# Attention rows with the second bias inside the exponential, key halves added before the sums, and a new order within a row

## The chip, the core and the metric

The kernel runs on one core of one Trainium2 chip. The metric is the device time of one execution in microseconds (us): the median of three runs before the change is 3339.98 us (3334.67 to 3347.28).

A core has five engines with queues of their own: TensorE (PE in the profile; its weight loads are PEld), VectorE (DVE), ScalarE (ACT), GpSimd (POOL) and SyncE (SP), which here issues most of the transfers. Each engine works through its instructions in order; semaphores make one wait for another. PE writes to PSUM; DVE and ACT read PSUM and SBUF, POOL works on SBUF tiles here.

## The reference

The model has two layers. The change concerns layer 0 alone, which is attention along rows with a gate. `x` and `kv_x` are 256 x 256 x 128 (rows s, positions, channels), with 4 heads of 32 channels:

```python
q = split_heads(einsum('...qi,oi->...qo', q_x, wq)) / sqrt(32)   # q_x is the group-normalised x
k = split_heads(einsum('...ki,oi->...ko', kv_x, wk))
v = split_heads(einsum('...ki,oi->...ko', kv_x, wv))
a = einsum('bshqd,bshkd->bshqk', q, k)
a = a + bias1 + bias2           # bias1: (1, 1, 4, 256, 256); bias2: (1, 256, 1, 1, 256)
a = softmax(a, axis=-1)
o = einsum('bshqk,bshkd->bshqd', a, v)
g = sigmoid(einsum('...qi,oi->...qo', q_x, wg) + bg)
x = x + einsum('...qi,oi->...qo', o * g, wo) + bo
```

`bias1` depends on head, query and key and is the same for all rows; `bias2` depends on row and key. The group normalisation needs statistics over all of `x` before the first row. Layer 1 then works on the result with Fourier transforms, a second attention and several normalisations.

## The kernel before

**Stages.** `layer0` first loads `x` in 32 blocks of 1 MB, transposes them on PE and takes statistics on DVE (L113, L114), sums them up (L116 to L119), and then calls `layer0_rows`. That one first prepares the biases: it loads `bias1` and `bias2` (L170, L172), takes their largest and smallest values for a later test (L174, L175), transposes them (L180, L191), and leaves `b1T` (keys on the partitions; heads 0 and 1 as they are, heads 2 and 3 already through the exponential) and `eb2`, the exponential of `bias2` times a constant. The test at the end (L124 to L146) sends the whole layer through a slow general branch when a bias is out of its limits or the result isn't finite.

**A row.** The row loop goes over 256 rows. Row `i` passes through steps that are spread over several iterations, so that iteration `i` issues `scores(i)`, `turn(i+2)`, `project(i+1)`, `attend(i-1)`, `out(i-2)` and `spectrum(i-3)`:

- `load`: two rows of `x` and `kv` at a time, on SP's queue (tiles `xt`, `kt`), four rows or more ahead.
- `turn`: PE transposes both (tile `tr`); ACT writes `xnT` (L219, normalised) and `kvT` (L221).
- `project`: PE makes queries and keys (tile `qk`) and gate and values (tile `gv`); ACT copies `qkT` (L230), DVE writes `v`, the values times `eb2` (L240), ACT the gate by a tanh (L244).
- `scores`: 8 small matmuls with 32 rows each, one for each head and key half (tiles `sc`, two PSUM tiles with one buffer each). Heads 2 and 3 go through ACT's exponential (L261) and are then multiplied by the exponential of `bias1` on POOL (L263); heads 0 and 1 get `bias1` added by DVE (L262, reading PSUM) and then ACT's exponential (L264). Each of these works on 1024 elements per partition.
- `attend`: 8 matmuls with the values, and 8 with `eb2` in the place of the values, which give the softmax's sums (tile `av`, L275). A matmul of this type stands in the profile as two records. DVE multiplies by the gate (L281) and takes the reciprocal of the sums (L282); POOL multiplies the two (`og`, L284) and adds the output bias to `x` (`xb`, L287).
- `out`: PE projects (tile `wo`), DVE adds `xb` (L297), SP stores the row (L300).
- `spectrum`: PE transposes the row and multiplies it by a Fourier matrix (tile `u`); DVE takes statistics (L311), ACT copies the spectrum to `U` (L312).

**What sets the order.** The program writes the order out by hand; a scheduler places the instructions in each engine's queue by their dependencies, and inserts the semaphores. PSUM tiles `tr`, `qk`, `gv`, `av`, `wo` and `u` share a pool of four buffers that go round in the order in which they are asked for: a tile can be written when the tile four before it has been read out. SP's queue holds loads of later rows and stores of earlier ones in one order.

Of the kernel before, what the change touches and what calls it, by code (L numbers as in the profile page):

```python
# [63 lines left out]
DEN_SCALE = 2.0 ** -69  # L64
BIAS_MAX, BIAS_MIN = 12.0, -40.0


def layer0(tc, I, C, ident, x1d, U, stats2):

# [8 lines left out]
    with ExitStack() as ctx:  # L78
        const = ctx.enter_context(tc.tile_pool(name="l0c", bufs=1))
        wT = {}  # L80
# [3 lines left out]
        nc.sync.dma_start(bg, I["L0_conv_bg"].unsqueeze(1))  # L84
        bad = const.tile([P, 4], FP, name="bad")
        adft = const.tile([P, 2, 129], FP, name="adft")
        nc.sync.dma_start(adft, C["adft"].rearrange("(p j) f -> p j f", j=2))

        with tc.tile_pool(name="l0p", bufs=2) as pp, tc.tile_pool(
            name="l0pp", bufs=4, space=PSUM  # L90
        ) as ps_p:
            gavg = pp.tile([P, P], FP, name="gavg", bufs=1)
            nc.sync.dma_start(gavg, C["gavg"])
            for n in ("wq", "wk", "wv", "wg", "wo"):
                w = pp.tile([P, P], FP, tag="w", name="w_" + n)
                nc.sync.dma_start(w, I["L0_conv_" + n])
                ps = ps_p.tile([P, 512], FP, tag="a", name="wps_" + n)
                nc.tensor.transpose(ps[:, 0:P], w, ident)
                wT[n] = const.tile([P, P], FP, name="wT_" + n)
                if n == "wq":  # L100
                    nc.scalar.mul(wT[n], ps[:, 0:P], 1.0 / math.sqrt(32.0))
                else:
                    nc.scalar.copy(wT[n], ps[:, 0:P])

            stats = pp.tile([P, NS // 2, 6], FP, name="stats1", bufs=1)
            xr = x.rearrange("s q c -> (s q) c").rearrange("(b p n) c -> b p n c", p=P, n=16)
            for b in range(xr.shape[0]):
                xb = pp.tile([P, 16, P], FP, tag="xb", name=f"xb_{b}", bufs=4)
                nc.sync.dma_start(xb, xr[b])
                for t in range(4):  # L110
                    ps = ps_p.tile([P, 512], FP, tag="a", name=f"xps_{b}_{t}")
                    for k in range(4):
                        nc.tensor.transpose(ps[:, k * P : (k + 1) * P], xb[:, 4 * t + k, :], ident)  # L113
                    nc.vector.bn_stats(stats[:, b * 4 + t, :], ps)  # L114
            mv = pp.tile([P, 2], FP, name="mv1", bufs=1)
# [5 lines left out]
        layer0_rows(tc, I, ident, x1d, U, stats2, wT, mr, nmr, bg, adft, bad)  # L121

        with tc.tile_pool(name="l0f", bufs=1) as fp, tc.tile_pool(
# [7 lines left out]
            nc.vector.tensor_reduce(f[:, 1:2], bad[:, 0:2], AX.X, ALU.max)  # L131
            nc.vector.tensor_scalar(f[:, 1:2], f[:, 1:2], BIAS_MAX, None, ALU.is_le)
            nc.vector.tensor_reduce(f[:, 2:3], bad[:, 2:4], AX.X, ALU.min)
            nc.vector.tensor_scalar(f[:, 2:3], f[:, 2:3], BIAS_MIN, None, ALU.is_ge)
            nc.vector.tensor_mul(f[:, 0:1], f[:, 0:1], f[:, 1:2])
            nc.vector.tensor_mul(f[:, 0:1], f[:, 0:1], f[:, 2:3])
# [12 lines left out]
def layer0_rows(tc, I, ident, x1d, U, stats2, wT, mr, nmr, bg, adft, bad):  # L149
# [3 lines left out]
    nc = tc.nc  # L153
    x, kv = I["x"][0], I["L0_conv_kv_x"][0]
    NS = x.shape[0]
    SG = 2
    with ExitStack() as ctx:
        const = ctx.enter_context(tc.tile_pool(name="l0r", bufs=1))
        wo = const.tile([P, P], FP, name="wo_half")
        nc.vector.tensor_scalar(wo, wT["wo"], 0.5, None, ALU.mult)  # L160
        hbg = const.tile([P, 1], FP, name="hbg")
        nc.vector.tensor_scalar(hbg, bg, 0.5, None, ALU.mult)
        bo = const.tile([P, P], FP, name="bo")
        nc.sync.dma_start(bo, I["L0_conv_bo"].partition_broadcast(P))

        b1T = const.tile([P, 4, 2, 256], FP, name="b1T")
        eb2 = const.tile([P, 2, NS], FP, name="eb2")
        with tc.tile_pool(name="l0b", bufs=2) as bp, tc.tile_pool(name="l0bp", bufs=4, space=PSUM) as ps_b:
            b1n = bp.tile([P, 4, 2, 256], FP, name="b1n", bufs=1)
            nc.sync.dma_start(b1n, I["L0_conv_bias1"][0, 0].rearrange("h (p j) k -> p h j k", j=2))  # L170
            b2n = bp.tile([P, 2, 256], FP, name="b2n", bufs=1)
            nc.sync.dma_start(b2n, I["L0_conv_bias2"][0, :, 0, 0, :].rearrange("(j p) k -> p j k", p=P))  # L172
            for k, (op, at) in enumerate(((ALU.max, 0), (ALU.min, 2))):
                nc.vector.tensor_reduce(bad[:, at : at + 1], b1n.rearrange("p h j k -> p (h j k)"), AX.X, op)  # L174
                nc.vector.tensor_reduce(bad[:, at + 1 : at + 2], b2n.rearrange("p j k -> p (j k)"), AX.X, op)  # L175
            for h in range(4):
                ps = ps_b.tile([P, 512], FP, tag="a", name=f"b1ps_{h}")
                for c in range(2):
                    for j in range(2):
                        nc.tensor.transpose(  # L180
                            ps[:, (2 * c + j) * P : (2 * c + j + 1) * P], b1n[:, h, j, c::2], ident
                        )
                dst = b1T[:, h].rearrange("p c q -> p (c q)")
                if h < 2:
                    nc.vector.tensor_copy(dst, ps)
                else:
                    nc.scalar.activation(dst, ps, AF.Exp)
            ps = ps_b.tile([P, 512], FP, tag="a", name="b2ps")
            for c in range(2):
                for j in range(2):  # L190
                    nc.tensor.transpose(  # L191
                        ps[:, (2 * c + j) * P : (2 * c + j + 1) * P], b2n[:, j, c::2], ident
                    )
            nc.scalar.activation(eb2.rearrange("p c s -> p (c s)"), ps, AF.Exp)
            nc.vector.tensor_scalar(eb2, eb2, DEN_SCALE, None, ALU.mult)

        ld = ctx.enter_context(tc.tile_pool(name="l0ld", bufs=2))
# [3 lines left out]
        rows = {}  # L201

        def load(g):
            s0 = g * SG
            xt = ld.tile([P, SG, 2, P], FP, tag="xt", name=f"xt_{g}", bufs=4)
            nc.sync.dma_start(xt, x[s0 : s0 + SG].rearrange("s (p j) c -> p s j c", j=2))
            kt = ld.tile([P, SG, 2, P], FP, tag="kt", name=f"kt_{g}")
            nc.sync.dma_start(kt, kv[s0 : s0 + SG].rearrange("s (p j) c -> p s j c", j=2))
            for i in range(SG):
                rows[s0 + i] = {"x": xt[:, i], "kv": kt[:, i]}  # L210

        def turn(s):
# [6 lines left out]
            nc.scalar.activation(r["xnT"], ps[:, 0:256], AF.Identity, bias=nmr, scale=mr[:, 1:2])  # L219
# [3 lines left out]
        def project(s):  # L223
# [8 lines left out]
            for c in range(2):  # L232
# [5 lines left out]

            r["v"] = wk.tile([P, 2, P], FP, tag="v", name=f"v_{s}", bufs=3)
            nc.vector.tensor_tensor(  # L240
                r["v"], ps[:, 256:512].rearrange("p (c d) -> p c d", c=2), bc(eb2[:, :, s], 2, P), ALU.mult
            )
            r["gate"] = wk.tile([P, 256], FP, tag="gate", name=f"gate_{s}", bufs=3)
            nc.scalar.activation(r["gate"], ps[:, 0:256], AF.Tanh, bias=hbg, scale=0.5)  # L244
# [74 lines left out]
        for i in range(NS + 3):  # L319
# [6 lines left out]
            if i + 1 < NS:  # L326
                project(i + 1)
# [1190 lines left out]
```

## Time and profile before

| what | us |
|---|---|
| median of three runs | 3339.98 |
| the profiled execution, its own time | 3339.29 |
| its span in the profile | 3337.5 |
| statistics of `x`: last DVE statistic ends | 95.02 |
| first transpose of a row starts | 119.84 |
| last `U` copy of a row ends | 1812.83 |
| layer 1, the rest of the span | 1524.7 |

Busy time over the span, from the first part of the page: PE 2903.5 (87%), DVE 1874.7 (56%), ACT 1258.2 (38%), POOL 1107.9 (33%). These shares are means over stages. In the second part, the span is cut into 40 slices of 83 us, one digit each for tenths of busy time:

```
PE   7799999999999999999997795879976595688666
DVE  8566666666666666666666215736563253355344
ACT  0355555555555555555553101010001431244022
POOL 0255555555555555555553002000000700000001
PEclk9899999999999999999998975889987797799766
```

The rows are slices 2 to 22. There PE is busy all the time (9 means 90% or more), the others about half. Idle time of an engine that isn't the bottleneck costs nothing; so what counts in the rows is what PE does and what makes it wait.

Costliest groups of the row loop (256 of each per execution, except where noted; mean of one in ns): the reciprocal L282 on DVE, 1750; the multiply L263 on POOL, 2382; the bias add L262 on DVE, 1206; the exponentials L261 and L264 on ACT, 1060 and 1078; the gate multiplies L281 on DVE, 421, and L284 on POOL, 728.

### The profile page before, as it was taken

How to read it: one execution, taken by the hardware profiler on the slowest of the kernel's cores; microseconds unless marked ns; L12 is line 12 of the kernel's file. 1: busy time of each engine (PE TensorE's matmuls, PEld its weight loads, DVE VectorE, ACT ScalarE, POOL GpSimd, SP SyncE). 2: the span in 40 equal slices, each digit the busy share in tenths (PEclk: the TensorE clock that was granted, in tenths of full speed). 3: DMA queues.
4: the chain of work that ended last, by engine and by line, in shares of the span. 5: the costliest groups of instructions: out<-in, count | busy, mean ns of one | idle time of the engine just before them, and what ended most of it. 6: DMA issues, size and time to landing. Idle time of an engine off the chain costs nothing. (4 is left out here: it accounts for less than half of the span.)

```text
span 3337.5 us, 71936 instructions
## 1 busy us (share of the span) xinstructions
PE 2903.5 (87%) x30049; PEld 1942.7 (58%) x30049; DVE 1874.7 (56%) x2852; ACT 1258.2 (38%) x2293; POOL 1107.9 (33%) x919
## 2 busy tenths in 40 slices
PE   7799999999999999999997795879976595688666
PEld 6577777777777777777775474744433244333443
DVE  8566666666666666666666215736563253355344
ACT  0355555555555555555553101010001431244022
POOL 0255555555555555555553002000000700000001
PEclk9899999999999999999998975889987797799766
DMA  9221221222221221222120000077633924887398
GB/s 378 96 63 59 63 63 60 61 63 60 61 63 60 62 63 60 61 63 61 60 63 27 1 8 13 0 277 251 226 129 125 312 74 113 269 308 275 86 358 319
DMA packets 237710, 401.71 MB, mean 120 GB/s; under 512 B 25125, under 2 KB 184312, under 8 KB 223304
## 3 DMA queue, kind: packets, MB, share of 16 engines
q1 hardware_dynamic: 221832, 329.97, 30.7%
q0 software_dynamic: 12672, 46.14, 3.5%
q10 hardware_dynamic: 2880, 20.97, 1.5%
q8 instruction: 238, 3.90, 0.5%
q14 instruction: 88, 0.72, 0.1%
HBM read 261.20 MB, written 135.79 MB: 119 GB/s over the span
## 5 line engine op out<-in xcount | busy, mean ns | idle before, releaser
L263 POOL TENSOR_TENSOR e<-e,b1T 128x1024 f32<-128x1024 f32 x256 | 609.8, 2382 | 103.7 <-ACT e L261 103.5
L282 DVE RECIPROCAL rd<-av 128x256 f32<-128x256 f32 x256 | 448.1, 1750 | 0.0
L284 POOL TENSOR_TENSOR og<-t,rd 128x256 f32<-128x256 f32 x256 | 186.4, 728 | 611.7 <-PE sc L253 593.5
L312 ACT COPY U<-u 128x129 f32<-128x129 f32 x256 | 99.3, 388 | 719.3 <-DVE stats L311 719.3
L281 DVE SCALAR_TENSOR_TENSOR t<-gate,av 128x256 f32<-128x256 f32 x256 | 107.7, 421 | 401.0 <-ACT gate L244 383.4
L262 DVE TENSOR_TENSOR e<-sc,b1T 128x1024 f32<-128x1024 f32 x256 | 308.8, 1206 | 2.7 <-PE sc L253 2.6
L253 PE MATMUL sc<-qkT 32*128 32x256 f32 x4096 | 293.4, 400 | 0.1
L264 ACT ACTIVATE e<-e 128x1024 f32<-128x1024 f32 x256 | 276.0, 1078 | 0.5 <-DVE e L262 0.4
L275 PE MATMUL av<-e,v 128*32 128x256 f32 x4096 | 274.7, 385 | 0.5 <-POOL e L263 0.5
L261 ACT ACTIVATE e<-sc 128x1024 f32<-128x1024 f32 x256 | 271.4, 1060 | 4.0 <-PE sc L253 3.8
L275 PE MATMUL av<-e,eb 128*32 128x256 f32 x4096 | 268.2, 379 | 0.0
L1025 PE MATMUL yps<-xt,mpT 128*128 128x512 f32 x512 | 230.3, 603 | 13.3 <-DMA xt<-x1d 13.3
L1351 POOL DMA_DIRECT2D out_dram<-x x64 | 34.1, 533 | 621.1 <-DVE x L1350 314.6
L287 POOL TENSOR_TENSOR xb<-xt,bo 128x256 f32<-128x256 f32 x256 | 187.5, 733 | 118.9 <-DMA kt<-in_L_conv_kv_x_dram 118.9
L240 DVE TENSOR_TENSOR v<-gv,eb 128x256 f32<-128x256 f32 x256 | 108.9, 425 | 198.3 <-PE gv L237 198.2
L1187 POOL TENSOR_TENSOR ww<-ww,xw 128x1024 f32<-128x1024 f32 x24 | 56.4, 2351 | 493.1 <-DMA xw<-x1d 482.3
L253 PEld LDWEIGHTS sc<-qkT 32*128 32x128 f32 x4096 | 185.0, 184 | 37.9 <-issue 0.7
L293 PEld LDWEIGHTS wo<-wo_half,og 128*128 128x128 f32 x1024 | 133.5, 190 | 107.0 <-issue 104.2
L275 PEld LDWEIGHTS av<-e,eb 128*32 128x32 f32 x4096 | 133.0, 110 | 88.2
L293 PE MATMUL wo<-wo_half,og 128*128 128x128 f32 x1024 | 182.4, 301 | 1.9 <-POOL og L284 1.9
L275 PEld LDWEIGHTS av<-e,v 128*32 128x32 f32 x4096 | 106.8, 109 | 129.7 <-ACT xnT L219 80.5
L1025 PEld LDWEIGHTS yps<-xt,mpT 128*128 128x128 f32 x512 | 95.4, 191 | 125.6 <-issue 113.6
(599 smaller groups left out, 5479.5 us busy)
## 6 DMA issues: line engine op xcount, KB each, us to landing
xb<-in_x_dram SPq DMA_DIRECT2D x32, 1024.0 KB
xt<-in_x_dram SPq DMA_DIRECT2D x128, 256.0 KB
kt<-in_L_conv_kv_x_dram SPq DMA_DIRECT2D x128, 256.0 KB
x1d<-x SPq DMA_DIRECT2D x256, 128.0 KB
xt<-x1d SPq DMA_DIRECT2D x32, 1024.0 KB
out_dram<-x POOLq DMA_DIRECT2D x64, 512.0 KB, 7.6
yd<-yt ACTq DMA_DIRECT2D x20, 1024.0 KB
x<-x1d SPq DMA_DIRECT2D x40, 512.0 KB
```

The lines of the kernel that those rows point to most:

```text
L240: nc.vector.tensor_tensor(r["v"], ps[:, 256:512].rearrange("p (c d) -> p c d", c=2), bc(eb2[:, :, s], 2, P), ALU.mult)
L253: nc.tensor.matmul(sc[h // 2][:, h % 2, c * 256 : (c + 1) * 256], qkT[p, 256 + c * P : 256 + (c + 1) * P], qkT[p, 0:256], start=True, stop ...
L261: nc.scalar.activation(e[1], s1[1], AF.Exp)
L262: nc.vector.tensor_tensor(e[0], s1[0], b1[0], ALU.add)
L263: nc.gpsimd.tensor_tensor(e[1], e[1], b1[1], ALU.mult)
L264: nc.scalar.activation(e[0], e[0], AF.Exp)
L275: nc.tensor.matmul(ps[hd, den * 256 : (den + 1) * 256], w, r["e"][h // 2][:, h % 2, c, :], start=(c == 0), stop=(c == 1),)
L282: nc.vector.reciprocal(rd, ps[:, 256:512])
L284: nc.gpsimd.tensor_tensor(r["og"], t, rd, ALU.mult)
L287: nc.gpsimd.tensor_tensor(r["xb"], r["x"], bc(bo, 1, 2), ALU.add)
L293: nc.tensor.matmul(ps[:, j * P : (j + 1) * P], r["og"][:, j * P : (j + 1) * P], wo, start=True, stop=True)
L1025: nc.tensor.matmul(ps[j].rearrange("p (n w) -> p n w", w=W), mpT[:, sc, tt], by_turn(xt[:, sc])[:, j], start=(sc == 0), stop=False,)
```

## The change

The bias handling is turned round. All four heads are treated alike: ACT's exponential takes `bias2` as its bias, a value for each partition (key), so that each 1024-wide exponential becomes two 512-wide ones, one for each key half, and `b1T` holds the exponential of `bias1` (times a constant) for all heads. A new step, `weigh`, multiplies the exponentials by it, heads 2 and 3 on POOL, heads 0 and 1 on DVE, and then adds the two key halves (`es`). The sums in `attend` are then 4 matmuls with a tile of ones instead of 8 with `eb2`. The values are only copied (L256 of the new kernel). The last gate multiply goes from POOL to DVE (L309), in place into `og`, and the addition of the output bias writes `x1` directly (L312). Constants keep the numbers in range: 2^-46 in `b1T`, 2^34 in the gate multiply, the rest in `wo`.

In an iteration the order is now `scores(i)`, `turn(i+2)`, `project(i+1)`, `weigh(i)`, `out(i-3)`, `spectrum(i-4)`, `attend(i-1)`, and the loop has one more turn. The PSUM pool still has four buffers. The biases' limits are taken from `b1T` in rows 8 to 15 (8 reduces on DVE), and `bias2` has no limits any more. The preparation (transposes, exponentials, copies) and the loads of the weights are moved into the loop over the 32 blocks of `x`, and the first four rows' loads stand behind it. The class `Rows` holds what were local variables. The diff, cut to its core:

```diff
-DEN_SCALE = 2.0 ** -69
-BIAS_MAX, BIAS_MIN = 12.0, -40.0
+E_SCALE, SUM_SCALE = 2.0 ** -46, 2.0 ** 34
+WO_SCALE = 0.5 / SUM_SCALE
+BIAS_MAX, BIAS_MIN = 24.0, -40.0
...
+                if b == 2:
+                    nc.sync.dma_start(gavg, C["gavg"])
...
+                    for n in ("wq", "wk", "wv", "wg", "wo"):
+                        w = pp.tile([P, P], FP, tag="w", name="w_" + n)
+                        nc.sync.dma_start(w, I["L0_conv_" + n])
...
+                if b == 8:
+                    rows.prepare(pp, ps_p)
+            rows.load(0)
+            rows.load(1)
...
+    def prepare(self, bp, ps_b):
+        nc, I, ident = self.tc.nc, self.I, self.ident
+        nc.gpsimd.memset(self.ones, 1.0)
...
+            dst = self.b1T[:, h].rearrange("p c q -> p (c q)")
+            nc.scalar.activation(dst, ps, AF.Exp)
+            nc.gpsimd.tensor_scalar(dst, dst, E_SCALE, None, ALU.mult)
...
+        nc.scalar.copy(self.b2T.rearrange("p c s -> p (c s)"), ps)
...
-            nc.vector.tensor_tensor(
-                r["v"], ps[:, 256:512].rearrange("p (c d) -> p c d", c=2), bc(eb2[:, :, s], 2, P), ALU.mult
-            )
+            nc.vector.tensor_copy(r["v"].rearrange("p c d -> p (c d)"), ps[:, 256:512])
...
-            nc.scalar.activation(e[1], s1[1], AF.Exp)
-            nc.vector.tensor_tensor(e[0], s1[0], b1[0], ALU.add)
-            nc.gpsimd.tensor_tensor(e[1], e[1], b1[1], ALU.mult)
-            nc.scalar.activation(e[0], e[0], AF.Exp)
+            for hp in (1, 0):
+                for c in range(2):
+                    nc.scalar.activation(
+                        r["e"][hp][:, :, c, :], sc[hp][:, :, c * 256 : (c + 1) * 256],
+                        AF.Exp, bias=b2T[:, c, s : s + 1],
+                    )
+
+        def weigh(s):
...
+            for hp, eng in ((1, nc.gpsimd), (0, nc.vector)):
+                e = r["e"][hp]
+                e1 = e.rearrange("p h c q -> p (h c q)")
+                eng.tensor_tensor(e1, e1, b1T[:, 2 * hp : 2 * hp + 2].rearrange("p h c q -> p (h c q)"), ALU.mult)
+                eng.tensor_tensor(r["es"][hp], e[:, :, 0, :], e[:, :, 1, :], ALU.add)
...
+            for h in range(4):
+                nc.tensor.matmul(
+                    ps[32 * h : 32 * h + 32, 256:512], self.ones, r["es"][h // 2][:, h % 2, :],
+                    start=True, stop=True,
+                )
...
             nc.vector.reciprocal(rd, ps[:, 256:512])
-            r["og"] = wk.tile([P, 256], FP, tag="og", name=f"og_{s}")
-            nc.gpsimd.tensor_tensor(r["og"], t, rd, ALU.mult)
+            nc.vector.scalar_tensor_tensor(t, rd, SUM_SCALE, t, ALU.mult, ALU.mult)
...
-        for i in range(NS + 3):
+        for i in range(NS + 4):
...
+            if i < NS:
+                weigh(i)
+            if 8 <= i < 16:
+                k, h = divmod(i - 8, 4)
+                nc.vector.tensor_reduce(
...
+            if 0 <= i - 3 < NS:
+                out(i - 3)
+            if 0 <= i - 4 < NS:
+                spectrum(i - 4)
+                del rows[i - 4]
             if 0 <= i - 1 < NS:
                 attend(i - 1)
-            if 0 <= i - 2 < NS:
-                out(i - 2)
-            if 0 <= i - 3 < NS:
-                spectrum(i - 3)
-                del rows[i - 3]
```

The line numbers of the new kernel's steps that the prediction names: L236 `xnT`, L238 `kvT`, L247 `qkT`, L258 gate, L275 the exponentials, L287 the multiplies by `b1T`, L288 the added halves, L307 to L309 gate and reciprocal, L322 `x1`, L336 statistics, L337 `U`.

## The prediction

> **What bounds the kernel now.** I read four views, in this order: the busy times by stretch (which stage, which engine), the timeline of one row (what waits for what), the groups (durations), and the timelines of a later stage where GpSimd and VectorE work side by side. In the first view the columns after the length are PE, PEld, DVE, ACT and POOL busy, then granted clock, DMA share and GB/s.
>
> ```profile
> 400.00:800.00 400.00, 400.00 (x4387) 288.00 (x4386) 258.14 (x366) 228.50 (x426) 230.68 (x182) 1.00 0.20 61
> ```
>
> TensorE has no idle time in the row loop, at full clock; DVE works 65%, ACT 57%, POOL 58%. One row, from the timeline (start, duration, engine, line):
>
> ```profile
> 1002.37 1.15 PE L253 MATMUL sc<-qkT 32*128 32x256 f32 x16
> 1003.45 0.33 PE L216 MATMUL tr<-ident,xt 128*128 128x128 f32 x1
> 1004.22 1.06 ACT L261 ACTIVATE e<-sc 128x1024 f32<-128x1024 f32 x1
> 1005.17 0.56 ACT L219 ACTIVATE xnT<-tr,nmr,mr 128x256 f32<-128x256 f32 x1
> 1005.61 0.37 ACT L221 COPY kvT<-tr 128x256 f32<-128x256 f32 x1
> 1005.78 1.07 PE L275 MATMUL av<-e,v 128*32 128x256 f32 x16
> 1006.67 1.05 PE L275 MATMUL av<-e,eb 128*32 128x256 f32 x16
> 1006.82 0.59 ACT L230 COPY qkT<-qk 128x512 f32<-128x512 f32 x1
> 1007.29 0.51 ACT L244 ACTIVATE gate<-gv,hbg 128x256 f32<-128x256 f32 x1
> 1007.64 0.71 PE L293 MATMUL wo<-wo_half,og 128*128 128x128 f32 x4
> 1008.19 0.38 PE L306 MATMUL u<-ident,x 128*128 128x128 f32 x2
> 1008.95 1.15 PE L253 MATMUL sc<-qkT 32*128 32x256 f32 x16
> ```
>
> A row is 1008.95 - 1002.37 = 6.58 us. From start to start PE spends 1.08 on the scores, 0.49 on transposes, 1.84 on projections (1003.94 to 1005.78), 0.89 on values, 0.97 on sums, 0.55 on `wo` and 0.76 on `u`. Note kvT: it ends at 1005.98, and the matmul that takes over its PSUM buffer, `wo`, starts 1.66 later. Durations for the new work:
>
> ```profile
> L263 POOL TENSOR_TENSOR e<-e,b1T 128x1024 f32<-128x1024 f32 x256 | 609.8, 2382 | 103.7 <-ACT e L261 103.5
> L287 POOL TENSOR_TENSOR xb<-xt,bo 128x256 f32<-128x256 f32 x256 | 187.5, 733 | 118.9 <-DMA kt<-in_L_conv_kv_x_dram 118.9
> L1064 DVE TENSOR_TENSOR xm_11r<-F,mixwr 128x1024 f32<-128x1024 f32 x1 | 1.2, 1226 | 0.5 <-PE xacc L1067 0.5
> L1064 DVE TENSOR_TENSOR z0m_10r<-F,mixwr 128x512 f32<-128x512 f32 x1 | 0.7, 693 | 0.2 <-PE z0acc L1067 0.2
> ```
>
> And two engines beside each other, in layer 1:
>
> ```profile
> 2041.54 0.40 DVE L820 TENSOR_SCALAR qt<-Xlo,kwi,hs 128x256 f32<-128x256 f32 x1
> 2043.59 0.46 DVE L823 SCALAR_TENSOR_TENSOR qf<-Xlo,kwr,qt 128x256 f32<-128x256 f32 x1
> 2043.97 1.13 DVE L820 TENSOR_SCALAR qt<-Xlo,kwi,hs 128x256 f32<-128x256 f32 x1
> 2043.76 1.20 POOL L851 TENSOR_TENSOR pr<-pr,st 128x512 f32<-128x512 f32 x1 [0.70 <-DVE st L850]
> L826 POOL TENSOR_SCALAR qt<-Xlo,kwr x16: 914/954/1405, 2027.7 to 2070.5; 128x256 f32<-128x256 f32 x16
> ```
>
> The same DVE operation takes 0.40 alone and 1.13 when a two-input POOL operation runs: it ends 0.14 after POOL. POOL's L851 takes 1.04 alone and 1.20 when it starts under a two-input DVE operation (L823); POOL's L826 grows from 0.91 to 1.41. Against a full block: most two-input DVE operations beside L826 kept their 0.47 (the longest 0.69), but L826 has only one tensor input.
>
> **The change, part by part, in the row loop.** *Removed on PE:* half the sums' matmuls (16 to 8 records). At 0.97 for 16 that is 0.49; without waits a row would be 6.09.
>
> *ACT:* two 1024-wide exponentials become four 512-wide ones with a per-partition bias. No row has this. From gate (256 wide, such a bias) 0.51, plus 256 elements by qkT and kvT (0.59 - 0.37 = 0.22): 0.73. The low bound is half of the present 1.06, 0.53. I take 0.73, since gate has the same operand. Neighbours overlap by 0.11 or so (qkT lasts 0.59, gate starts 0.47 after it), so a step is 0.62. ACT's sum becomes 4 x 0.73 + 0.56 + 0.37 + 0.59 + 0.51 + 0.39 = 5.34, below the row.
>
> *DVE:* the bias multiply reads SBUF twice, 1.23 in place of 1.21; the added halves 0.69; the last gate multiply comes from POOL, 0.47 (as L823); the value copy stays at 0.43. Sum 0.42 + 1.75 + 0.47 + 1.23 + 0.43 + 0.69 + 0.36 + 0.42 = 5.77 instead of 4.58. Eight reduces of 0.68 in rows 8 to 15 lie in its spare time; if not, they cost 5 us once.
>
> *POOL:* 2.38 + halves + 0.73. The halves at 512 are 1.04 by L851 or 1.28 on the line through 256 and 1024; I take 1.16: 4.27.
>
> *Order and constants:* `wo` now runs three rows late and stands ahead of `av`; its buffer is that of the `av` two rows back, whose reciprocal ends about 2.3 after the scores' start (0.42 + 1.75), while `wo` is reached at 3.41 (1.08 + 0.49 + 1.84): nothing. The folded scales remove two small operations outside the rows: nothing.
>
> By busy time all this fits under 6.09. Two waits do not.
>
> *Wait one, a PSUM buffer.* Four buffers go round over tr, qk, gv, wo, u, av, so `u` now takes tr's buffer of the same iteration and waits for kvT; ACT's instruction order puts kvT behind all four exponentials (before, one stood ahead of it). Behind `u` in PE's queue stand `av` and the next scores. The circle: scores to first exponential 1.18 (row two: 130.30 to 131.48), four steps 2.48, xnT 0.44, kvT 0.37, wake 0.05, `u` with its weight load 0.87 (1008.08 to 1008.95), values 0.89, sums 0.49: 6.77. So the 0.49 saved on PE turns into 0.68 of waiting.
>
> *Wait two, SBUF access of DVE and POOL.* In the row loop of before, every DVE operation reads at least one operand from PSUM. Now three (1.23, 0.69, 0.47) read two tensors from SBUF, while POOL reads SBUF for 4.27 of a row. What they cost each other is not shown for these pairs: from nothing to full exclusion. The Trainium skill, page "SBUF — State Buffer", section "SBUF: two separate sides", says that a VectorE operation with two SBUF inputs and a GpSimd operation that reads SBUF exclude each other for the whole instruction; by that the row would be 8.14 and the time some 3728. The rows above (0.40 to 1.13, 1.04 to 1.20) are nearer to exclusion than to nothing, but show the waiting one catching up some 0.25 before the other's end (it ends 0.14 after POOL, though it lasts 0.40). So I take exclusion less 0.25 at each of the two hand-overs from POOL to DVE.
>
> The circle with exclusion: exponentials one and two 0.62 + 0.73, wake 0.05; POOL's multiply 2.38; DVE's gate multiply and bias multiply, stuck behind it in DVE's queue, 0.40 + 1.15 (their steps); POOL's halves, next in its queue, 1.16; DVE's halves 0.61; then on DVE x1 0.28 and statistics 0.42; U on ACT waits for the statistics, 0.06 + 0.28; the next exponentials stand behind U. Sum 8.14; less 0.50: 7.64. Wait one then has slack. Against 6.58: +1.06 x 256 = +271 us; unshortened, 8.14 would give +399, and 3728.
>
> *Outside the rows.* Bias preparation leaves the path. Before:
>
> ```profile
> 83.74 11.24 DVE L114 BATCH_NORM_STATS2 stats<-xps 128x6 f32<-128x512 f32 x18
> 111.29 2.29 DVE L174 TENSOR_REDUCE bad<-b1n 128x1 f32<-128x2048 f32 x1 [6.87 <-DMA b1n<-in_L_conv_bias_dram]
> 119.84 0.66 PE L216 MATMUL tr<-ident,xt 128*128 128x128 f32 x2 [2.87 <-DMA xt<-in_x_dram]
> ```
>
> From 103.94 to 119.84, 15.9 us go: loads of bias and first rows now run under or just behind the statistics (rows 0 to 3 add four loads to SP's queue behind the last `xb`). Given back: the exponential's table load, 1.28, now among the first rows; and the statistics, which run with DVE full (18 in 11.24) and DMA at 1.00. 1.25 MB of bias at 410 GB/s is 3 us, and PE, in order, waits for weights loaded two at a time between big loads (such a wait was 6 us, 4.77 to 11.02). The first `xb` is issued 2.35 earlier, and PE waits for no weight before it. I take 3 us net: -15.9 + 1.3 + 3 = -12, from -19 to -5. The tail has one more turn, +1. POOL's four scalings and memset find its queue empty until the rows. In SP's queue both kt and xt loads are two rows or more ahead; kt behind two stores costs nothing unless a row lags by two.
>
> Sum: 3337.5 + 271 - 12 + 1 = 3597.5 span. The profiled run took 1.8 more than its span and the median is 0.7 above it: 3600.
>
> **Rivals.** *No exclusion worth the name:* wait one decides, 6.77: +49 - 11 gives 3378. For it: two-input DVE operations at 0.47 beside L826. Against: 1.13 and 1.41. *Faster, the exponentials are short:* if a 512 piece costs 0.53 (step 0.42), wait one's circle is 5.97, PE's 6.09 decides, and without exclusion the time is 3337.5 - 125 - 11 + 2.5 = 3204. It turns faster from a step under 0.58. For it: 1.06 for 1024; against: gate's 0.51 for 256. *It doesn't do what it says:* the fallback branch runs (a flag off by the new scales); bias exponentials of unit normal data lie far inside both limits, so nearly excluded.
>
> **Numbers.** Exclusion 0.70 (slower); no exclusion 0.17 (0.12 slower, 0.03 same, 0.02 faster); short exponentials 0.12; fallback 0.01. Slower 0.83, same 0.03, faster 0.14; 0.5% is 17 us, about what a measurement can tell. The range holds 7.64 and both sides: up to 3705 (just short of full exclusion), down to 3360 (no exclusion, step 0.60). The likeliest case's own range is 3460 (7.1 a row: hand-overs of 0.5) to 3728.
>
> **What would show it.** A row of 7.6 us; DVE L287 and L288 or POOL L287 and L288 longer than 1.23, 0.69, 2.38 and 1.16 when they overlap; PE idle before `wo` or `av`; ACT's exponentials released by PE right after U. If DVE L287 is 1.23 everywhere and PE waits at `u` for kvT (L238), rival one holds. ACT L275 at 0.53 would make me wrong, and so would a PE busy at 100%.

## The result, and the profile after

The changed kernel takes 3747.27 us (median of 4 runs, 3737.42 to 3751.0) against 3337.32 us for the kernel before (4 runs beside them, 3333.06 to 3347.28): a ratio of 1.1219, 95% interval 1.1185 to 1.1253, so it is 12% slower. The forecast was 3600, slower, with a range from 3360 to 3705: the sign was right, and the time lies above the range.

| | before | after | difference |
|---|---|---|---|
| span of the profiled run | 3337.5 | 3749.2 | +411.7 |
| first scores start | 125.7 | 115.5 | -10.2 |
| first scores to last `U` (256 rows) | 1687.1 | 2103.5 | +416.4 |
| behind the last `U` | 1524.7 | 1530.2 | +5.5 |

The rows have all of it, 416.4 / 256 = 1.63 us each. The last line is scatter: in the other runs of this study that stretch, whose code is untouched, took between 1517 and 1531.

The busy times by stretch, the same 400 us that were shown of before (length, then PE, PEld, DVE, ACT, POOL busy, granted clock, DMA share, GB/s):

```profile
400.00:800.00 400.00, 327.01 (x3127) 221.00 (x3119) 398.33 (x392) 208.01 (x438) 260.32 (x147) 1.00 0.16 49
```

TensorE went from 100% to 82%, VectorE from 65% to 99.6%, at the same clock. It would be wrong to read that VectorE is now short of throughput: 392 instructions fill 398 us where 366 filled 258, and the groups say which of them grew (busy us and mean ns behind the bar):

```profile
L287 POOL TENSOR_TENSOR e<-e,b1T 128x1024 f32<-128x1024 f32 x256 | 601.9, 2351 | 707.2 <-ACT e L275 692.1
L275 ACT ACTIVATE e<-sc,b2T 128x512 f32<-128x512 f32 x1024 | 618.2, 695 | 1.1 <-PE sc L267 0.9
L287 DVE TENSOR_TENSOR e<-e,b1T 128x1024 f32<-128x1024 f32 x256 | 588.4, 2298 | 4.5 <-ACT e L275 4.5
L309 DVE SCALAR_TENSOR_TENSOR og<-rd,og 128x256 f32<-128x256 f32 x256 | 546.5, 2135 | 8.7
L312 POOL TENSOR_TENSOR x<-xt,bo 128x256 f32<-128x256 f32 x256 | 431.6, 1687 | 67.0 <-DVE mr L127 67.0
...
L288 POOL TENSOR_TENSOR es<-e 128x512 f32<-128x512 f32 x256 | 345.3, 1349 | 20.0
...
L288 DVE TENSOR_TENSOR es<-e 128x512 f32<-128x512 f32 x256 | 224.4, 877 | 0.0
```

VectorE's multiply was priced at 1.23 alone and takes 2.30; `og` was priced at 0.47 and takes 2.14; GpSimd's x + bo, 0.73, takes 1.69. An instruction that is blocked counts as busy here: the wait stands inside its duration, not in the idle column behind it. The timeline of one row shows in what order they block each other (start, duration, engine, line):

```profile
1003.22 2.41 ACT L275 ACTIVATE e<-sc,b2T 128x512 f32<-128x512 f32 x4
1004.55 2.35 POOL L287 TENSOR_TENSOR e<-e,b1T 128x1024 f32<-128x1024 f32 x1 [2.77 <-ACT e L275]
1005.03 2.16 DVE L309 SCALAR_TENSOR_TENSOR og<-rd,og 128x256 f32<-128x256 f32 x1
1006.98 1.34 POOL L288 TENSOR_TENSOR es<-e 128x512 f32<-128x512 f32 x1
1007.11 2.30 DVE L287 TENSOR_TENSOR e<-e,b1T 128x1024 f32<-128x1024 f32 x1
1008.29 1.70 POOL L312 TENSOR_TENSOR x<-xt,bo 128x256 f32<-128x256 f32 x1
1009.33 0.41 DVE L256 COPY v<-gv 128x256 f32<-128x256 f32 x1
1009.66 0.88 DVE L288 TENSOR_TENSOR es<-e 128x512 f32<-128x512 f32 x1
1010.47 0.41 DVE L322 TENSOR_TENSOR x<-wo,x 128x256 f32<-128x256 f32 x1
1010.80 0.41 DVE L336 BATCH_NORM_STATS2 stats<-u 128x6 f32<-128x256 f32 x1
1011.25 0.39 ACT L337 COPY U<-u 128x129 f32<-128x129 f32 x1 [0.99 <-DVE stats L336]
1011.43 2.42 ACT L275 ACTIVATE e<-sc,b2T 128x512 f32<-128x512 f32 x4
```

A row is 1011.43 - 1003.22 = 8.21 us. Read the ends: GpSimd's multiply ends at 1006.90, `og` behind it at 1007.19, GpSimd's halves at 1008.32, VectorE's multiply at 1009.41, GpSimd's x + bo at 1009.99, VectorE's halves at 1010.54. They are six operations in strict turns, POOL, DVE, POOL, DVE, POOL, DVE. Their own lengths are 2.35, 0.40, 1.26, 1.23, 0.73 and 0.68, in all 6.65 (1.26 is a multiply of this size on GpSimd by itself, in the run on the hand-over below; 0.73 is x + bo in the kernel before, and 0.68 VectorE's halves in the runs below that nothing blocks); the six take 1010.54 - 1004.55 = 5.99. The difference, 0.66, lies in the five changes of engine, 0.11 to 0.15 at each. Around the six stand 1.33 (two exponentials ahead) and 0.89 (x1, statistics, `U`, up to the next exponential): 5.99 + 1.33 + 0.89 = 8.21.

Ahead of the rows, VectorE's timeline of the changed kernel:

```profile
21.55 0.70 DVE L105 BATCH_NORM_STATS2 stats<-xps 128x6 f32<-128x512 f32 x1 [6.60 <-PE xps L104]
...
39.50 0.69 DVE L355 TENSOR_REDUCE bad<-b1T 128x1 f32<-128x512 f32 x1 [3.02 <-POOL b1T L201]
...
102.31 3.62 DVE L125 BATCH_NORM_AGGREGATE mv<-stats 128x2 f32<-128x768 f32 x1
```

The first statistics start 8.4 earlier than before (6.91 against 15.33) and yet the last end 7.3 later (102.31 against 95.02). Between lie a wait of 6.6, in which TensorE stood at the transposes of late weights (2.4 for the load of `wv`, 4.1 for that of `wo`), waits of 5.7 for GpSimd's scaling of `b1T`, and the eight reduces, 5.4, which the compiled order has among the statistics although they are written into rows 8 to 15. From the last statistics to the first scores it is now 13.2 instead of 30.7.

### The profile page after: what moved, and what is told of

Read it like the earlier page. It is cut to its first block, busy times and chain, and to the rows that moved or that the text cites. A ratio compares the mean times of both kernels' runs of the same rounds, so it can differ in the third digit from the quotient of the medians.

```text
span 3749.2 us, 69101 instructions
## 1 busy us (share of the span) xinstructions
PE 2954.1 (79%) x28001; PEld 1903.9 (51%) x28001; DVE 2868.9 (77%) x3363; ACT 1390.4 (37%) x2808; POOL 1509.8 (40%) x924
## 5 line engine op out<-in xcount | busy, mean ns | idle before, releaser
L287 POOL TENSOR_TENSOR e<-e,b1T 128x1024 f32<-128x1024 f32 x256 | 601.9, 2351 | 707.2 <-ACT e L275 692.1
L275 ACT ACTIVATE e<-sc,b2T 128x512 f32<-128x512 f32 x1024 | 618.2, 695 | 1.1 <-PE sc L267 0.9
L287 DVE TENSOR_TENSOR e<-e,b1T 128x1024 f32<-128x1024 f32 x256 | 588.4, 2298 | 4.5 <-ACT e L275 4.5
L309 DVE SCALAR_TENSOR_TENSOR og<-rd,og 128x256 f32<-128x256 f32 x256 | 546.5, 2135 | 8.7
L312 POOL TENSOR_TENSOR x<-xt,bo 128x256 f32<-128x256 f32 x256 | 431.6, 1687 | 67.0 <-DVE mr L127 67.0
L258 ACT ACTIVATE gate<-gv,hbg 128x256 f32<-128x256 f32 x256 | 121.5, 475 | 745.2 <-DVE v L256 745.1
L288 POOL TENSOR_TENSOR es<-e 128x512 f32<-128x512 f32 x256 | 345.3, 1349 | 20.0
L318 PE MATMUL wo<-wT_wo,og 128*128 128x128 f32 x1024 | 175.7, 294 | 108.0 <-DVE rd L308 103.3
L233 PE MATMUL tr<-ident,xt 128*128 128x128 f32 x512 | 140.5, 301 | 125.8 <-ACT gate L258 125.5
L318 PEld LDWEIGHTS wo<-wT_wo,og 128*128 128x128 f32 x1024 | 134.3, 191 | 203.4 <-PE gv L254 196.6
L288 DVE TENSOR_TENSOR es<-e 128x512 f32<-128x512 f32 x256 | 224.4, 877 | 0.0
L337 ACT COPY U<-u 128x129 f32<-128x129 f32 x256 | 98.0, 383 | 263.3 <-DVE stats L336 263.3
```

Of the source, the lines that this page charges most:

```text
L233: nc.tensor.transpose(ps[:, j * P : (j + 1) * P], r["x"][:, j, :], ident)
L275: nc.scalar.activation(r["e"][hp][:, :, c, :], sc[hp][:, :, c * 256 : (c + 1) * 256], AF.Exp, bias=b2T[:, c, s : s + 1],)
L287: eng.tensor_tensor(e1, e1, b1T[:, 2 * hp : 2 * hp + 2].rearrange("p h c q -> p (h c q)"), ALU.mult)
L288: eng.tensor_tensor(r["es"][hp], e[:, :, 0, :], e[:, :, 1, :], ALU.add)
L309: nc.vector.scalar_tensor_tensor(t, rd, SUM_SCALE, t, ALU.mult, ALU.mult)
L312: nc.gpsimd.tensor_tensor(r["x1"], r["x"], bc(self.bo, 1, 2), ALU.add)
```

## The experiments

Two theories stood against each other for most runs: that VectorE's operations with two SBUF tensors and GpSimd's exclude each other and this circle sets the row, or that the PSUM buffer (wait one of the prediction) or VectorE's own work does. Unless a ratio is given, a time is that of a single run; a row is read from the starts of one instruction in successive rows.

**GpSimd's share out.**

```diff
-            for hp, eng in ((1, nc.gpsimd), (0, nc.vector)):
+            for hp, eng in ((0, nc.vector),):
...
-                    ps[32 * h : 32 * h + 32, 256:512], self.ones, r["es"][h // 2][:, h % 2, :],
+                    ps[32 * h : 32 * h + 32, 256:512], self.ones, r["es"][0][:, h % 2, :],
```

> Left out: GpSimd's multiply by the first bias and its added halves for heads 2 and 3 (their sums are taken from the halves of heads 0 and 1). GpSimd keeps only x + bo (0.73 us a row alone). Theory (VectorE operations with two SBUF inputs and GpSimd exclude each other, and the circle through both engines sets the row of 8.21 us): the circle is gone, DVE L287 falls from 2298 ns to about 1230 and L309 from 2135 to about 400-500, and the row falls to what comes next, wait one's circle through kvT, 6.6 to 6.9 us; with 256 rows the time is 3749 - 256 x 1.4 = about 3390 (3350 to 3420). Rival A (the row is set by the PSUM buffer, u waiting for kvT behind four exponentials, and GpSimd is only beside it): the row stays near 8.2, 3700 or more. Rival B (VectorE itself is slower for these operations, whatever GpSimd does): L309 stays above 1.5 us and the row above 7.8.

Measured: 3348.41, row 6.68. Its groups:

```profile
L287 DVE TENSOR_TENSOR e<-e,b1T 128x1024 f32<-128x1024 f32 x256 | 313.6, 1225 | 257.9 <-ACT e L275 257.9
...
L331 PE MATMUL u<-ident,x 128*128 128x128 f32 x512 | 112.1, 301 | 128.4 <-ACT kvT L238 128.4
```

VectorE's multiply is back at 1225 ns (and `og` at 426) though nothing was changed on VectorE, and what is left is `u` waiting 0.5 a row for kvT. The row is near the 6.77 that the prediction had for wait one alone. But this run also takes work away, so the next one keeps it all.

**The same work, with one SBUF operand on VectorE.** The exponentials of heads 0 and 1 and the reciprocal are written over their own inputs in PSUM, and the halves are added by a reduction over pairs of one tensor.

```diff
-                        r["e"][hp][:, :, c, :], sc[hp][:, :, c * 256 : (c + 1) * 256],
+                        r["e"][hp][:, :, c, :] if hp else q, q, AF.Exp, bias=b2T[:, c, s : s + 1],
...
-            rd = wk.tile([P, 256], FP, tag="rd", name=f"rd_{s}", bufs=1)
+            rd = ps[:, 256:512]
...
+                    eng.tensor_reduce(r["es"][hp], e.rearrange("p h c q -> p h q c"), AX.X, ALU.add)
```

> Same work and the same result, but VectorE's three operations each read one SBUF tensor and one PSUM tensor: the exponentials of heads 0 and 1 stay in their PSUM banks, the reciprocal is written in place in PSUM, and the halves of heads 0 and 1 are added by a reduction over pairs of one tensor. GpSimd works as much as before the edit. Theory (two SBUF inputs against GpSimd exclude each other): L287 on VectorE falls to about 1.2, L309 to about 0.45, GpSimd's L288 and L312 to 1.26 and 0.73, and the row to 6.6 to 7.0 (wait one, or VectorE's own sum), about 3350 to 3450. Rival B (any VectorE operation beside GpSimd is slowed, whatever it reads, or the operations are slow by themselves): row 7.8 or more, over 3640.

Measured: 3361.24, row 6.69. Its groups:

```profile
L289 POOL TENSOR_TENSOR e<-e,b1T 128x1024 f32<-128x1024 f32 x256 | 603.8, 2359 | 584.9 <-ACT e L276 584.9
...
L289 DVE TENSOR_TENSOR e<-sc,b1T 128x1024 f32<-128x1024 f32 x256 | 313.5, 1225 | 170.3 <-ACT sc L276 170.3
L291 POOL TENSOR_TENSOR es<-e 128x512 f32<-128x512 f32 x256 | 329.2, 1286 | 20.0
L314 DVE SCALAR_TENSOR_TENSOR og<-av,og 128x256 f32<-128x256 f32 x256 | 108.6, 424 | 8.6
```

GpSimd does as much as in the changed kernel, its multiply in the same length, and beside it VectorE's multiply takes 1225 ns instead of 2298 and `og` 424 instead of 2135. For these two the only difference is where one operand lies; the halves are another operation. So of the 386 us between this run and the changed kernel, none comes from a smaller amount of work (the reduction even takes 1243 ns where the added halves took 877). The run on the hand-over below shows the same with no kernel around it.

**Wait one alone removed.** The call of `turn(i + 2)` is put ahead of `scores(i)`.

```diff
-            if i < NS:
-                scores(i)
             if i + 2 < NS:
                 turn(i + 2)
+            if i < NS:
+                scores(i)
```

> Only the order in which one iteration is written changes: the transposes of row i+2 with xnT and kvT stand ahead of the scores and exponentials of row i, so that u no longer takes the buffer of a kvT that waits behind four exponentials. Theory (the circle through VectorE and GpSimd sets the row): the row stays at 8.2 (8.05 to 8.35), the time within 40 us of 3749, and the wait of u for kvT (145.7 us in all) goes away or moves. Rival A (wait one sets the row, or a good part of it): the row falls to 7.7 or less, 3620 or less.

Measured: 3724.2, row 8.09, and TensorE's wait at `u` for kvT is gone: wait one costs at most 0.11 a row as long as wait two stands. (The order of the turns is another here, so that even the 0.11 may not be its own.) One row of this kernel, VectorE and GpSimd:

```profile
1006.68 2.39 POOL L287 TENSOR_TENSOR e<-e,b1T 128x1024 f32<-128x1024 f32 x1 [2.36 <-PE gv L254]
...
1007.80 2.37 DVE L287 TENSOR_TENSOR e<-e,b1T 128x1024 f32<-128x1024 f32 x1 [0.94 <-ACT e L275]
...
1009.15 2.13 POOL L288 TENSOR_TENSOR es<-e 128x512 f32<-128x512 f32 x1
...
1010.42 1.41 DVE L288 TENSOR_TENSOR es<-e 128x512 f32<-128x512 f32 x1
```

The exponentials start earlier against `og` here, so VectorE's multiply is the one that waits while GpSimd's runs, and it goes first when that ends (1009.07); GpSimd's halves then take 2.13. In this row, too, the engine that has been waiting goes next.

**Both waits removed.** The two edits together, with the exponentials of heads 0 and 1 written first.

> The edit of the PSUM kernel and that of the order (transposes of row i+2 ahead of the scores of row i) together, with the exponentials of heads 0 and 1 written first: the same result, and neither wait in the row. Theory: both waits are gone, TensorE's own work sets the row at 6.1 to 6.4 us, the time is 3749 - 256 x (8.21 - 6.25) = about 3250 (3200 to 3300), below the kernel before the change (3337). If a VectorE or ScalarE circle of 6.6 is left, 3340; if only exclusion was removed and wait one was nothing, the same as the PSUM kernel alone.

Measured: 3277.57 (4 runs), ratio to before 0.9807, interval 0.9791 to 0.9823: faster than the kernel before. Stretch from 400 to 800:

```profile
400.00:800.00 400.00, 398.72 (x4041) 291.87 (x4040) 371.04 (x507) 276.86 (x570) 273.53 (x190) 1.00 0.22 64
```

TensorE is full again. The rows alternate (6.20 and 6.47 about 1000 us), with a mean of 6.34 where 6.25 had been taken. What makes the difference is taken up with the last run.

**GpSimd's share out and the new order.** This is to price wait one without wait two.

> Left out: GpSimd's multiply and added halves for heads 2 and 3, as in the run that left them out; and the transposes of row i+2 stand ahead of the scores of row i. Theory: with neither wait left, TensorE is the bound as the matmuls' sum has it, 6.1 to 6.25 us a row, about 3220 (3200 to 3255): the part of the 0.58 us a row above this in the run without GpSimd (6.68) is then all wait one. Rival (something else, VectorE's or ScalarE's own sum, holds the row at 6.6 or more): 3330 or more.

Measured: 3294.58, row 6.42: both theories miss. 0.26 of a row was wait one; behind it stands another wait, in one row of this kernel:

```profile
1004.89 0.42 DVE L256 COPY v<-gv 128x256 f32<-128x256 f32 x1
...
1005.34 0.47 ACT L258 ACTIVATE gate<-gv,hbg 128x256 f32<-128x256 f32 x1 [1.15 <-DVE v L256]
1005.86 0.14 PEld L233 LDWEIGHTS tr<-ident,xt 128*128 128x128 f32 x1 [0.60 <-ACT gate L258]
```

The gate waits for VectorE's copy of v, which stands behind VectorE's multiply, and the next transposes take the PSUM buffer that the gate frees. With less work than the run before it, this one is 17 us slower; the order of the exponentials is that of the changed kernel here, with those for VectorE last.

**GpSimd's added halves alone out.**

```diff
-                eng.tensor_tensor(r["es"][hp], e[:, :, 0, :], e[:, :, 1, :], ALU.add)
+                if hp == 0:
+                    eng.tensor_tensor(r["es"][hp], e[:, :, 0, :], e[:, :, 1, :], ALU.add)
```

> Left out: GpSimd's added halves for heads 2 and 3 alone (their sums are taken from the halves of heads 0 and 1). Theory (GpSimd and VectorE take turns, and whoever is next in the other engine's queue goes at once): x + bo takes the place of the halves in the turn, so the row falls by 1.26 - 0.73 there, and by some 0.2 more because VectorE's own halves then meet nothing: 7.45 us (7.3 to 7.6), about 3555 (3515 to 3595). Rival (the halves are not on the circle, as they lie behind both of VectorE's multiplies and are hidden by them): row 8.0 to 8.2, 3700 or more. Second rival (the order of the prediction, in which both of VectorE's multiplies go ahead and the halves' whole length stands on the circle): the row falls by 1.16 or more, to 7.0, about 3440.

Measured: 3477.69, row 7.18: below the theory's range of 7.3 to 7.6, and above the 7.0 of the second rival. x + bo did not take the place of the halves, because it was not ready when GpSimd's multiply ended at 1006.07:

```profile
1006.27 1.21 DVE L287 TENSOR_TENSOR e<-e,b1T 128x1024 f32<-128x1024 f32 x1
1006.48 1.60 POOL L313 TENSOR_TENSOR x<-xt,bo 128x256 f32<-128x256 f32 x1 [0.41 <-PE u L334]
```

It waited 0.41 for `u` (the buffer it writes), so VectorE's multiply followed `og` unblocked. The row still fits the turns; what the expectation had overlooked is a wait. From GpSimd's multiply to VectorE's halves it is 2.35 + 0.40 + 1.21 + 0.73 + 0.68 = 5.37 by lengths and 4.90 in the trace: 0.12, 0.13 and 0.14 less at the three changes of engine, and 0.08 where VectorE's multiply follows `og` on its own engine.

**The hand-over by itself.** The kernel before, with a stretch of its own ahead: operations on 512 elements, VectorE's 16 beside GpSimd's 8, after each alone.

> The kernel before the change, with a stretch of its own ahead of everything: operations of 512 elements a partition, first each alone (8 times), then VectorE's (16) beside GpSimd's (8). Theory (operations with two SBUF tensors on VectorE and GpSimd's exclude each other for their length, less about 0.13 us at each hand-over, and they take turns): VectorE's multiply alone 0.60 a step, GpSimd's 1.26; side by side a pair of them takes 0.60 + 1.26 - 0.26 = 1.60; with one operand in PSUM nothing changes on either side (0.60 and 1.26); the reduction over one SBUF tensor is not slowed either; a multiply of one SBUF tensor by a constant is slowed, as VectorE's L820 was in layer 1 (0.40 to 1.13). Credit of the prediction (0.25 for each hand-over from GpSimd to VectorE, nothing back): a pair 1.61, but with GpSimd's at 1.26 and VectorE's alone shortened. Rival (no exclusion): VectorE's steps stay at 0.60 in every pair and 16 of them take 10 us.

Timeline of that stretch (one line is 8 or 16 instructions; L1486 two SBUF tensors, L1489 one in PSUM, L1492 one SBUF tensor times a constant, L1495 reduction; GpSimd's L1498 two tensors, L1501 one):

```profile
5.10 5.78 DVE L1486 TENSOR_TENSOR mb_c<-mb_a,mb_b 128x512 f32<-128x512 f32 x8 [0.35 <-ACT mb_b L1508]
...
29.06 10.64 POOL L1498 TENSOR_TENSOR mb_f<-mb_d,mb_e 128x512 f32<-128x512 f32 x8 [27.28 <-ACT mb_e L1508]
...
53.79 19.12 DVE L1486 TENSOR_TENSOR mb_c<-mb_a,mb_b 128x512 f32<-128x512 f32 x16 [25.70 <-ACT mb_b L1508]
54.09 13.19 POOL L1498 TENSOR_TENSOR mb_f<-mb_d,mb_e 128x512 f32<-128x512 f32 x8 [0.98 <-ACT mb_e L1508]
...
73.67 11.56 DVE L1489 TENSOR_TENSOR mb_c<-mb_z,mb_b 128x512 f32<-128x512 f32 x16 [0.76 <-ACT mb_b L1508]
73.97 10.68 POOL L1498 TENSOR_TENSOR mb_f<-mb_d,mb_e 128x512 f32<-128x512 f32 x8 [6.69 <-ACT mb_e L1508]
```

With two SBUF tensors, eight pairs take turns: a pair takes 1.67 us from one start of GpSimd's to the next (8 of them 13.19), where the lengths alone are 0.69 and 1.26, together 1.95. That is 0.14 saved at each hand-over, in both directions; the 1.60 that was expected had taken 0.60 for VectorE's 0.69. With one operand in PSUM both engines run at the speed they have alone (11.56 is twice 5.78, 10.68 against 10.64).

**x + bo out.**

```diff
-            nc.gpsimd.tensor_tensor(r["x1"], r["x"], bc(self.bo, 1, 2), ALU.add)
...
-                r["x1"], ps[:, 0:256].rearrange("p (j c) -> p j c", j=2), r["x1"], ALU.add
+                r["x1"], ps[:, 0:256].rearrange("p (j c) -> p j c", j=2), r["x"], ALU.add
```

> Left out: GpSimd's x + bo (x alone is added to wo's result, so bo is missing). Theory (strict turns: GpSimd's multiply, og, GpSimd's halves, VectorE's multiply, GpSimd's x + bo, VectorE's halves, each with its own length less about 0.13 at a hand-over; the prediction's circle left x + bo out): VectorE's halves no longer wait, L288 on VectorE falls from 877 to about 680 ns, and what stands between the multiply and the halves is then VectorE's copy of v, 0.25: the row falls by 0.20 to 8.01, the time to about 3700 (3685 to 3715). Rival (x + bo lies behind the circle, as the prediction had it): the row stays at 8.21, 3740 or more.

Measured: 3692.98, row 8.01, VectorE's halves 681 ns.

**x + bo out, and the copy of v on ScalarE.** As the run above, with `nc.scalar.copy` for `nc.vector.tensor_copy` in `project`.

> As the run without x + bo, and the copy of v moves from VectorE to ScalarE. Left out: bo. Theory: now nothing of what the prediction's circle lacked stands in it; a step of 0.33 more goes from VectorE's part, the row falls to 8.21 - 0.20 - 0.33 = 7.68, next to the 7.64 of the prediction, and the time to about 3615 (3595 to 3640). Rival (the credit for early release was the error, and the circle's terms were complete): the row stays at 8.0 or more, 3690 or more.

Measured: 3603.34, row 7.68. VectorE and GpSimd in one row of it:

```profile
1003.27 1.35 POOL L288 TENSOR_TENSOR es<-e 128x512 f32<-128x512 f32 x1
1003.40 2.30 DVE L287 TENSOR_TENSOR e<-e,b1T 128x1024 f32<-128x1024 f32 x1
1005.62 0.41 DVE L321 TENSOR_TENSOR x<-wo,xt 128x256 f32<-128x256 f32 x1
1005.96 0.68 DVE L288 TENSOR_TENSOR es<-e 128x512 f32<-128x512 f32 x1
```

With these two out of the circle the kernel is the one that the prediction described, and its time is the predicted one to 3 us. So close a hit is in part luck: the three hand-overs of this row are worth 0.38 (0.11, 0.12 and 0.15), and not the 0.50 of the credit, and smaller terms make up for it.

**The stretch ahead of the rows mended**, on the kernel with both waits removed: a buffer for each weight, and the reduces of the bias write a tile of the rows' own pool, which puts them behind the statistics.

```diff
-                        w = pp.tile([P, P], FP, tag="w", name="w_" + n)
+                        w = pp.tile([P, P], FP, tag="w", name="w_" + n, bufs=5)
...
+        bad = wk.tile([P, 2, 4], FP, name="badr", bufs=1)
```

> The kernel with both waits removed (3277.57), and two things mended ahead of the rows: the five weights get a buffer each, so that no transpose on TensorE waits for the load of a weight behind the big loads (6.6 us of VectorE's idle time at 22 us), and the eight reduces of the bias that stood among the statistics (8 x 0.6 us, and 5.5 us of waits for GpSimd's scaling) move behind them, to where VectorE waits for the first gv. Theory: statistics end 102.3 - 6.6 - 10 = about 86, at earliest 90 if the loads (33.5 MB at some 420 GB/s, from 2 us on, with 1.6 MB of bias and weights) set the end; first scores 10 to 13 us earlier, 3265 (3258 to 3272). Rival (the loads set the end already): 3274 to 3279, no change.

Measured: 3271.97 (5 runs), ratio to before 0.9797, interval 0.9781 to 0.9813. The intervals of this run and of the one with both waits removed overlap, so the times alone do not tell them apart; in the profile the first scores start at 110.6 instead of 117.2. The gain is 6.6 of the 10 to 13 expected, since waits for loads took the place of those removed: in this kernel TensorE stands 3.0 us for the load of an `xb` up to 16.65, and 1.8 for that of `bias1` up to 34.14, and VectorE's statistics stand behind it.

**VectorE's reduction behind the statistics**, on the kernel above: the reduction of the halves is written behind `spectrum(i - 4)`.

> The best kernel so far (3271.97) with VectorE's reduction of the halves moved behind x1 and the statistics of u in its queue. Reading of that kernel's trace: its rows alternate between 6.20 and 6.46 us, and the 6.46 is a circle through VectorE and ScalarE: multiply, x1, reduction (1.14), statistics, U, four exponentials with qkT between them, next multiply; the reduction stands between the multiply and U. Theory: with the reduction behind the statistics the circle falls to about 5.8 and TensorE's own 6.2 sets the row: 3272 - 256 x (6.335 - 6.21) = 3240 (3232 to 3250). Rival (VectorE's sum with the small gaps at its waits sets 6.3, whatever the order): 3262 to 3275.

Measured: 3273.89 (5 runs), ratio 0.9799, interval 0.9781 to 0.9817: no change, the rows still alternate (6.51 and 6.16 about 1000 us, mean 6.34). So the circle that was read from the trace was not what sets the 6.34. Where the time goes stands in TensorE's queue, in this kernel and in the one with both waits removed alike. Each of its steps has the same length in every row (within 0.1) but one, from `wo` to `u`: 0.44 to 0.78, mean 0.58 and 0.59. In the long ones `u` starts 0.06 after the end of VectorE's `og` (kernel with both waits removed, a long row and a short one):

```profile
1001.40 0.61 PE L323 MATMUL wo<-wT_wo,og 128*128 128x128 f32 x4
1001.62 0.42 DVE L314 SCALAR_TENSOR_TENSOR og<-av,og 128x256 f32<-128x256 f32 x1
1002.11 0.44 PE L336 MATMUL u<-ident,x 128*128 128x128 f32 x2
...
1007.86 0.61 PE L323 MATMUL wo<-wT_wo,og 128*128 128x128 f32 x4
1008.31 0.43 PE L336 MATMUL u<-ident,x 128*128 128x128 f32 x2
```

So the 6.34 is 6.20 of TensorE's own steps and 0.14 of waiting for `og`, which in these kernels reads the reciprocal in PSUM; in the run with GpSimd's share out and the new order, where the reciprocal lies in SBUF, the step is 0.44 in every row. Why `og` is late in every second row is open (VectorE is 93% busy), and no run removes this wait alone.

## Why the prediction was right in sign and wrong in size

- *Nothing is saved on TensorE as long as a wait sets the row:* right, TensorE is 18% idle. What the sums' matmuls save is 0.43 and not 0.49: from their start to the next step it is 0.55 now, 0.97 before.
- *Wait one, 6.77:* right. With wait two gone it sets 6.68 (GpSimd's share out) and 6.69 (operands in PSUM); beside wait two it costs at most 0.11 (8.21 with it, 8.09 without).
- *Wait two, exclusion:* right, and shown by the kernel with operands in PSUM and by the pairs of operations alone. The rule of the Trainium skill that the prediction weighed, page "SBUF — State Buffer", section "SBUF: two separate sides", was nearer than the correction made to it: 3728 by the rule, 3747 measured, 3600 forecast. That nearness is partly luck. Over the six operations that in fact take turns, blocking for their whole lengths would give a row of 6.65 + 1.33 + 0.89 = 8.87; measured is 8.21, so an operation gets in 0.11 to 0.15 before the other's recorded end.
- *The circle with exclusion, 8.14 less 0.50:* this is the step that failed, by 0.57 a row, which is 145 of the 152 us that the forecast span lacks. Its main error is a term put at nothing: x + bo, 0.73, which the prediction had only in GpSimd's sum. Less 0.16 of hand-overs that it did not count, this is the 0.57. In three parts: (1) GpSimd's x + bo is missing from the circle, and so is VectorE's copy of v, which runs beside x + bo in the changed kernel and shows only where x + bo is out. The prediction let VectorE's two multiplies go one after the other; in the trace the engines take turns, and x + bo comes between VectorE's multiply and its halves. Taking it out gives 0.20; taking the copy of v out too, 0.53 in all: rows of 7.68 against the 7.64 predicted. (2) The credit of 0.25 for each of two hand-overs from GpSimd to VectorE was too large: each is worth 0.11 to 0.15 (the 0.25 was read from another operation, in layer 1). But there are five, in both directions, 0.66 in all, so the credit as a whole was not too large. (3) The small terms: the halves on GpSimd 1.26 and not 1.16, VectorE's multiply and halves 1.23 and 0.68 and not 1.15 and 0.61, the rest of the circle 2.22 and not 2.44 (1.40 and 1.04 in the prediction). These nearly cancel. That the uncorrected sum, 8.14, lies next to 8.21 is in part such a cancellation.
- *An exponential of 512 at 0.73, step 0.62:* 0.695 and 0.57. Rival "short exponentials", 0.53 with a step of 0.42, falls. The 0.57 lies just under the 0.58 from which the prediction had it turn faster without exclusion, and yet the rows of wait one alone, 6.68 and 6.69, are slower than before: by its sum they would be 6.57, so its other terms were 0.11 too short.
- *Ahead of the rows -12:* -10.2, but not by its terms. The statistics end 7.3 later and not 3, because the reduces do not lie in the spare time of rows 8 to 15: the scheduler moved them ahead, where they cost 5.4 and waits of 5.7. Against that, the stretch from the last statistics to the first scores shrank by 17.5, where 14.6 was forecast (15.9 less the table load's 1.3).
- *`wo` three rows late costs nothing:* no run shows a cost beside the circle. TensorE's idle time ahead of `wo`, 108 us in all, is released by the reciprocal, which is itself late by VectorE's turns; with GpSimd's share out it is 3.3.
- *TensorE's own 6.09:* without its wait for `og`, TensorE's steps add up to 6.20 in the kernel with both waits removed; single rows of the fastest kernels came down to 6.14, their mean stayed at 6.34.

## What to carry to other kernels

Before work is moved to VectorE beside a busy GpSimd, list for each operation which of its tensors lie in SBUF: those with two tensors there, and multiplies of one by a constant, were blocked here. If both engines have such operations waiting in the same stretch, write them down in turns, with every GpSimd operation of the period among them, and add up their lengths; do not go by each engine's sum. One operand left in PSUM took the multiply and `og` out of the turns, at their own lengths. Here that, with the halves added by a reduction, brought the loss from 12% to under 1%; with the transposes issued first as well there was a gain of 2%. It may have a price of its own: TensorE's wait for `og` was seen only in kernels in which `og` reads the reciprocal in PSUM.

## What the runs showed of the hardware

- A blocked operation is recorded as busy for the whole of its wait: VectorE at 99.6% did work for about 250 of 400 us in the changed kernel's stretch, if its three blocked operations are counted at their lengths alone (1.07, 1.74 and 0.20 a row less, at 48.7 rows).
- The blocking does not need two tensors. Beside GpSimd's two-tensor operation, VectorE's multiply of one SBUF tensor by a constant takes turns with it, 16 in 14.96 us where 8 alone take 3.65, while the reduction over one SBUF tensor is not touched (16 in 11.50, 8 alone in 5.73):

```profile
18.05 3.65 DVE L1492 TENSOR_SCALAR mb_c<-mb_a 128x512 f32<-128x512 f32 x8 [0.64 <-ACT mb_a L1508]
...
85.90 14.96 DVE L1492 TENSOR_SCALAR mb_c<-mb_a 128x512 f32<-128x512 f32 x16 [0.67 <-ACT mb_a L1508]
...
101.53 11.50 DVE L1495 TENSOR_REDUCE mb_c<-mb_a 128x256 f32<-128x512 f32 x16 [0.67 <-ACT mb_a L1508]
...
113.78 13.89 DVE L1486 TENSOR_TENSOR mb_c<-mb_a,mb_b 128x512 f32<-128x512 f32 x16 [0.76 <-ACT mb_b L1508]
114.00 14.00 POOL L1501 TENSOR_SCALAR mb_f<-mb_d 128x512 f32<-128x512 f32 x8 [1.43 <-ACT mb_e L1508]
```

  The Trainium skill, page "SBUF — State Buffer", section "Who interferes with whom", has both: multiplication by a scalar can enter a mode that takes the shared ports, a reduction cannot.
- The last two lines show the exception that made the prediction doubt the rule (L826 in layer 1): against a GpSimd operation with one tensor, VectorE's two-tensor operations are slowed only a little, 13.89 for 16 (11.6 alone), and GpSimd's 8 take 14.00 (12.49 alone), where exclusion would need 16 x 0.69 + 8 x 1.49 = 23. For this pair the rule that the prediction weighed does not hold as a full block.
